# Attention phase of a fused two-layer block: norms moved to ScalarE, loads of x pinned, weight stores set apart

## The chip, the cores and the metric

The program runs on one core of a Trainium2 chip. A core has TensorE (PE in the profile; its weight loads are listed as PEld), VectorE (DVE), ScalarE (ACT), GpSimd (POOL) and SyncE (SP), each with its own instruction queue that is worked off in order, and 16 DMA engines that all queues share. The metric is the time on the device in microseconds (us); lower is better. All data is float32.

## The reference, cut to what matters

Eight batches of 512 tokens with 512 features go through four residual blocks. This case touches the first two.

```python
# B=8 batches, S=512 tokens, D=512; 16 heads of 32; context of 64 tokens per batch
x = x + tanh(g_xattn[0]) * L0_xattn(layernorm(x), ctx, Wq, Wg, bg, Wkv, Wo)
x = x + tanh(g_ffn[0])   * L0_ffn(layernorm(x), proj1, b1, proj2, b2)
x = x + tanh(g_xattn[1]) * L1_xattn(layernorm(x), ctx, mask)
x = x + tanh(g_ffn[1])   * L1_ffn(layernorm(x), gate_weight, gate_up, down, ...)

def layernorm(x): return (x - mean(x)) / sqrt(var(x) + 1e-5)

def L0_xattn(query, kv, ...):          # linear attention
    q = features(query @ Wq.T); gate = sigmoid(query @ Wg.T + bg)
    k, v = split(kv @ Wkv.T);   k = features(k)   # x+1 where x>0, else exp(x)
    summary = einsum('bhsd,bhse->bhde', k, v); k_sum = k.sum(tokens)
    attn = (q @ summary) / (q @ k_sum + 1e-6)
    return attn * gate @ Wo.T
def L0_ffn(x, ...): return gelu(x @ proj1.T + b1) @ proj2.T + b2   # 512 -> 2048 -> 512
```

## The kernel before

The program is one long, fully unrolled list of instructions. A scheduler of the framework orders each engine's instructions by a simulation, unless the kernel pins them: the set `in_order` names the engines whose instructions, as long as they are in it, are kept behind the one traced last on the same engine (class `Ordered`, line 47 on). After the set-up (line 1321) TensorE, VectorE and ScalarE leave the set; GpSimd and SyncE stay in program order all through the attention phase.

**Matrix products** are done by a scheme with seven block products in place of eight (numbered 1 to 7). A product with a weight needs the four blocks of the weight and three differences of them, and likewise of the activations: `combining` (line 243) makes the weight's differences in place on VectorE or GpSimd, `token_combinations` (line 614) those of the normed tokens. `Unit.step(m)` issues one product of 8 matmuls (1.73 us) into an accumulator bank of PSUM and then the work that takes it out (`after`).

**Attention phase** (loop over b from line 1331). Per batch it traces seven products of `QUp` (query), seven of `GUp` (gate), and seven of `ODown` (output projection) of the batch before, since the two last products of a unit are issued late, after the first of the next unit (`steps`). Between them stand `denominators` (the products `pd`, a reciprocal in two halves, a store of `z` to DRAM as `over`, and its spreading load `spread` back over partitions), `numerators` (the 32 small matmuls `pn`, which fill four banks), `gated` (the tile `th`) and `attended` (the tile `a`, then its three combinations).

**Normed tokens.** While batch b is worked on, the generator `prep` of batch b+1 is pulled step by step by `some(prep)`. It is `normed` (line 463): bn_stats and bn_aggr for four tiles of 128 tokens, `var`, then `rstd` by a power on GpSimd (line 480), a yield; then for each tile the norm (`xn`, line 491, VectorE), its turning by four transposes on TensorE (`pt`, line 500), the copy to `xnT` by ScalarE (line 503), a yield. In the attention phase the first pull is at the fourth step of the gate's products, the others at steps 0, 1, 3 and 5 of ODown's.

**x's loads.** `load_x` (line 153) loads 1 MB of x for a batch. For batches 2 to 7 the queue is ScalarE's (line 164). They are traced at step 1 of the gate's products of the batch two before. `store_x` (line 173) writes the result of the attention back.

**Weights of the feed-forward blocks** are made during earlier phases by builders, generators that are pulled beside the products. `build_first` runs on GpSimd in the attention phase, one pull in two of five steps (`tick`); `build_second` runs on VectorE in the first feed-forward phase, one pull per up product, from line 440. Per tile: load raw weights, wait `LAND` pulls, combine in place, store, wait `GAP` pulls. For the down weights `combining_again` (line 370) takes a second level of differences in place: it stores three quarters at once (`keep`), then changes the tile step by step, and stores each changed quarter after its step. All these tiles share one buffer (`build_tile`). SyncE issues their loads and stores in program order with all other loads.

**Last batch.** At b = 7 the steps of `ODown(6)` also carry `gated` (steps 1 and 2) and `attended` (step 4) of batch 7, whose output projection follows at once, and the norms and turnings of the first feed-forward batch, pulled at steps 4, 5 and 6.

The order around the change at the end of a batch:

```python
for n, (u, m) in enumerate(steps([ODown(done[0])] if done else [])):
    u.step(m)
    in_order.discard("tensor")
    if b < B - 1:
        next(den, None)
        if n == 6:
            spread(b)
    elif n in (1, 2):
        gated(b, g.th, n - 1)
    elif n == 4:
        attended(b, g.th, pn)
    if n in ((0, 1, 3, 5) if b < B - 1 else (4, 5, 6)):
        some(prep)
    tick()
```

Of the kernel before, what the change touches and what calls it, by code (L numbers as in the profile page):

```python
# [68 lines left out]
def flamingo_kernel(  # L69
# [24 lines left out]
    nc = SimpleNamespace(**{e: Ordered(tc, e, in_order) for e in in_order})  # L94
    stack = ctx.enter_context
# [57 lines left out]
    def load_x(ph, b):  # L153
        if ph == "xa0" and b % 4 == 3:
            t = awork.tile([P, NT, D], F32, tag="x4", name=f"x_{ph}{b}")
        else:
            t = work.tile([P, NT, D], F32, tag="x", name=f"x_{ph}{b}", bufs=3)
        if ph == "xa0":
            src = x[ts(b, S), :].rearrange("(t p) d -> p t d", p=P)
        else:  # L160
            src = between[ph, b]

        queue = nc.scalar if ph == "xa0" and b > 1 else nc.sync
        queue.dma_start(out=t, in_=src)
        xs[ph, b] = t
# [204 lines left out]
    def combining_again(ph, i, t, eng):  # L370


        b = t.rearrange("p k n (h q) -> p k n h q", q=P)
        b11, b12, b21, b22 = (b[:, :, n, h] for n in range(2) for h in range(2))

        def keep(m, w):
            nc.sync.dma_start(out=stream[ph][:, :, SPLIT_INNER.index(m), i, :], in_=w)

        sub = ALU.subtract
        for m, w in ((1, b11), (2, b21), (3, b22)):  # L380
            keep(m, w)
        eng.tensor_tensor(b12, b12, b11, sub)
        yield
        keep(5, b12)
        eng.tensor_tensor(b22, b22, b12, sub)
        yield
        keep(6, b22)
        eng.tensor_tensor(b21, b21, b22, sub)
        yield
        keep(4, b21)  # L390
        eng.tensor_tensor(b11, b22, b11, sub)
        yield
        keep(7, b11)
# [5 lines left out]
    def build_first():  # L399
# [10 lines left out]
        for i in range(4):  # L410
# [13 lines left out]
            yield from combining_again("ff0", i, t, nc.gpsimd)  # L424
# [13 lines left out]
    LAND, GAP = 11, 6  # L438

    def build_second():  # L440
# [10 lines left out]
        for i in range(SPLIT_CHUNKS["ff1"]):  # L451
# [5 lines left out]
            yield from in_place(combining_again("ff1", i, t, nc.vector))  # L457
# [5 lines left out]
    def normed(ph, b, tag, normed_part=lambda t: None):  # L463
# [4 lines left out]
        ordered = ph == "ff0" and b > 1  # L468
        if ph == "xa0" or ordered:
            in_order.add("vector")  # L470
        for t in range(NT):
            st = small.tile([P, 6], F32, tag="st", name=f"st_{tag}_{t}")
            nc.vector.bn_stats(st, xb[:, t, :])
            nc.vector.bn_aggr(mv[:, t, :], st)
        if b:
            in_order.discard("vector")
        var = small.tile([P, NT], F32, tag="var", name=f"var_{tag}")
        nc.vector.tensor_scalar(var, mv[:, :, 1], LN_EPS, None, ALU.add)  # L478
        rstd = small.tile([P, NT], F32, tag="rstd", name=f"rstd_{tag}")
        nc.gpsimd.tensor_tensor(rstd, var, neg_half, ALU.pow)  # L480
        if ph in ("xa0", "ff0") or tag.startswith("ff1"):
            yield
# [4 lines left out]
        def norm(t):  # L487
            xn[t] = work.tile([P, D], F32, tag="xn", name=f"xn_{tag}_{t}")
            if ordered:
                in_order.add("vector")  # L490
            nc.vector.tensor_scalar(
                xn[t], xb[:, t, :], mv[:, t, 0:1], rstd[:, t : t + 1], ALU.subtract, ALU.mult
            )
            if ordered:
                in_order.discard("vector")
# [19 lines left out]
        if ordered:  # L515
            norm(0)
            yield
        for t in range(NT):
            if not ordered:
# [811 lines left out]
    for b in range(B):  # L1331
# [4 lines left out]
        for n, (u, m) in enumerate(steps([q])):  # L1336
# [5 lines left out]
            if n == 4:  # L1342
                flush()
            tick()
# [26 lines left out]
        for n, (u, m) in enumerate(steps([ODown(done[0])] if done else [])):  # L1371
            u.step(m)
# [5 lines left out]
            elif n in (1, 2):  # L1378
                gated(b, g.th, n - 1)
            elif n == 4:  # L1380
                attended(b, g.th, pn)
            if n in ((0, 1, 3, 5) if b < B - 1 else (4, 5, 6)):
                some(prep)
            tick()
        for _ in prep:
# [188 lines left out]
```

## Time and profile before

| What | Value |
|---|---|
| Median of three runs (lowest, highest) | 2095.27 us (2091.73, 2095.57) |
| The profiled execution, its time on the device | 2096.49 us |
| The same execution, span from first to last instruction | 2094.7 us |
| Busy: PE, PEld, DVE, ACT, POOL | 2053.7, 1821.1, 1511.3, 610.8, 171.1 us |
| Mean granted PE clock | 0.992 |
| Attention phase, from PE's first projection of x to the first product of the feed-forward block | 54.27 to 409.16 us |
| DVE `xn_xa` (line 491), 28 times between 54.27 and 353.58 | 33.9 us, mean 1232 ns |
| DVE bn_stats, bn_aggr there, 28 each | mean 667 and 181 ns |
| POOL `rstd_xa` there, 7 times | mean 1009 ns |
| POOL waits for stores of `build_ff_down` | 46.1 us, 3 times |

The busy times add up over engines that work side by side; only what PE waits for, or what runs while its granted clock is below 1, sets the end here. A line of the timeline gives the start in us, the duration, the engine, the line in the kernel, the operation, what it writes and reads, its shape and count, and in brackets how long the engine had been idle before it and what ended that. Where a helper records the instruction, its line is 60. "q" after an engine's name marks its instruction queue, for issues of DMA.

### The profile page before, as it was taken

What the parts mean: (1) busy time and instruction counts of PE and PEld (TensorE: products, weight loads), DVE (VectorE), ACT (ScalarE), POOL (GpSimd) and SP (SyncE); (2) the same over time, 40 slices, a digit from 0 to 9 for tenths busy, and PEclk for the clock granted to TensorE, in tenths of its full rate; (3) what the DMA queues carried; (4) which work ended last, traced back from release to release, by engine and by line L of the source; (5) the groups of instructions that cost most, each with busy time, mean ns of one, the idle gap of its engine ahead of it and who ended that gap; (6) DMA issues with size and microseconds to landing.
All of it is one profiled execution on the core that took longest, in us unless ns stands there. A gap on an engine that the chain in (4) does not pass through costs nothing.

```text
span 2094.7 us, 35097 instructions
## 1 busy us (share of the span) xinstructions
PE 2053.7 (98%) x12796; PEld 1821.1 (87%) x12796; DVE 1511.3 (72%) x2965; ACT 610.8 (29%) x1264; POOL 171.1 (8%) x164
## 2 busy tenths in 40 slices
PE   8999999999999999999999999999999999999998
PEld 4777887799999898989988989898989889898988
DVE  3688888657768576768767687777777676876758
ACT  3433333232332324232334222312222222223121
POOL 3233320100000000000001010000000010100000
PEclk9999999999999999999999999999999999999999
DMA  7354763598888887879786858586766858585865
GB/s 227 127 177 147 208 210 98 159 302 283 261 285 296 271 288 262 283 240 310 249 305 214 286 162 284 190 269 211 238 224 208 270 174 291 159 283 163 269 203 170
DMA packets 304170, 484.66 MB, mean 231 GB/s; under 512 B 36992, under 2 KB 103712, under 8 KB 299904
## 3 DMA queue, kind: packets, MB, share of 16 engines
q1 hardware_dynamic: 296560, 455.65, 68.2%
q10 hardware_dynamic: 5856, 23.20, 2.9%
q0 software_dynamic: 1584, 3.57, 0.7%
q8 instruction: 103, 1.69, 0.3%
q14 instruction: 67, 0.55, 0.1%
HBM read 413.04 MB, written 69.27 MB: 230 GB/s over the span
## 4 chain that ended last, share of the span: by engine, by line
PE 90%; DVE 4%; DMA 3%; issue 1%; POOL 1%; ACT 0%; SPq 0%; ACTq 0%; DVEq 0%; POOLq 0%
PE x_ff L840 26%; PE w_ff L840 13%; PE x_ff_down L1035 13%; PE w_ff_down L1035 8%; PE z_ff L840 6%; PE z_ff_down L1035 4%; PE v_ff_down L1035 4%; PE x_xa_down L956 2%; PE x_q L840 2%; PE pt_ff L500 1%; PE x_g L840 1%; PE pt_xa L500 1%; PE w_xa_down L956 1%; PE w_g L840 1%; DMA stream_ff<-build_ff_down 1%
## 5 line engine op out<-in xcount | busy, mean ns | idle before, releaser
L840 PE MATMUL w_ff<-S_ff,w_ff 128*128 128x256 f32 x1280 | 305.4, 381 | 4.2 <-DVE a_ff L895 4.2
L840 PE MATMUL x_ff<-S_ff,w_ff 128*128 128x256 f32 x1280 | 304.3, 380 | 0.0
L840 PE MATMUL x_ff<-xnT_ff,w_ff 128*128 128x256 f32 x1280 | 294.6, 379 | 0.0
L852 ACT COPY u_ff<-x_ff 128x512 f32<-128x512 f32 x240 | 140.0, 584 | 477.7 <-PE x_ff L840 453.1
L840 PEld LDWEIGHTS x_ff<-S_ff,w_ff 128*128 128x128 f32 x1280 | 240.5, 190 | 40.1 <-issue 5.0
L840 PEld LDWEIGHTS w_ff<-S_ff,w_ff 128*128 128x128 f32 x1280 | 240.0, 191 | 37.4 <-DVE a_ff L895 5.0
L840 PEld LDWEIGHTS x_ff<-xnT_ff,w_ff 128*128 128x128 f32 x1280 | 237.7, 190 | 31.1 <-ACT u_ff L852 0.5
L1035 PE MATMUL x_ff_down<-w_ff_down,split_ff_down 128*128 128x128 f32 x1344 | 157.9, 275 | 0.0
L1035 PEld LDWEIGHTS x_ff_down<-w_ff_down,split_ff_down 128*128 128x128 f32 x1344 | 153.9, 192 | 0.0
L840 PE MATMUL z_ff<-xnT_ff,w_ff 128*128 128x256 f32 x640 | 152.6, 381 | 0.0
L840 PEld LDWEIGHTS z_ff<-xnT_ff,w_ff 128*128 128x128 f32 x640 | 120.7, 192 | 15.8
L1049 DVE TENSOR_TENSOR part_ff_down<-part_ff_down 128x128 f32<-128x128 f32 x315 | 84.7, 288 | 64.5 <-ACT part_ff_down L1062 57.6
L1035 PE MATMUL w_ff_down<-w_ff_down,split_ff_down 128*128 128x128 f32 x896 | 105.3, 275 | 0.0
L1035 PEld LDWEIGHTS w_ff_down<-w_ff_down,split_ff_down 128*128 128x128 f32 x896 | 102.6, 192 | 0.0
L895 DVE TENSOR_TENSOR a_ff<-w_ff,u_ff 128x512 f32<-128x512 f32 x64 | 43.9, 687 | 69.6 <-ACT u_ff L852 69.5
L900 ACT ACTIVATE a_ff<-a_ff,b_sb 128x256 f32<-128x256 f32 x128 | 58.1, 501 | 97.6 <-DVE a_ff L895 97.6
L923 DVE SCALAR_TENSOR_TENSOR g_ff<-th_ff,x_ff 128x512 f32<-128x512 f32 x48 | 32.9, 685 | 70.3 <-ACT th_ff L922 70.3
L480 POOL TENSOR_TENSOR rstd_ff<-var_ff,neg_half 128x4 f32<-128x4 f32 x15 | 15.3, 1020 | 826.5 <-DVE var_ff L478 826.5
L1035 PE MATMUL w_ff_down<-w_ff_down,s_ff 128*128 128x128 f32 x672 | 81.5, 275 | 0.0
L1035 PE MATMUL x_ff_down<-w_ff_down,a_ff 128*128 128x128 f32 x672 | 80.4, 275 | 0.0
L1035 PEld LDWEIGHTS w_ff_down<-w_ff_down,s_ff 128*128 128x128 f32 x672 | 79.4, 192 | 0.8
L1035 PEld LDWEIGHTS x_ff_down<-w_ff_down,a_ff 128*128 128x128 f32 x672 | 78.4, 192 | 0.5
(254 smaller groups left out, 3450.4 us busy)
## 6 DMA issues: line engine op xcount, KB each, us to landing
w_ff_down<-stream_ff SPq DMA_DIRECT2D x680, 256.0 KB
w_ff<-ff_up SPq DMA_DIRECT2D x560, 256.0 KB
stream_ff<-build_ff_down SPq DMA_DIRECT2D x49, 448.0 KB
x_ff<-x_ff SPq DMA_DIRECT2D x16, 1024.0 KB
share<-shares SPq DMA_DIRECT2D x64, 256.0 KB
ff_up<-build_ff_up SPq DMA_DIRECT2D x42, 256.0 KB
spread<-over SPq DMA_DIRECT2D x32, 256.0 KB
x_ff<-x_xa ACTq DMA_DIRECT2D x8, 1024.0 KB
```

The costliest lines, as they stand in the source:

```text
L480: nc.gpsimd.tensor_tensor(rstd, var, neg_half, ALU.pow)
L500: nc.tensor.transpose(pt[:, c, :], xn[t][:, ts(c, P)], ident)
L840: nc.tensor.matmul(p[:, n, :], lhsT=w[:, c, ts(n, P)], rhs=moving, **self.mark(m, 2 * n + c),)
L852: nc.scalar.copy(self.s[m], p)
L895: nc.vector.tensor_tensor(h, p, s, ALU.add)
L900: nc.scalar.activation(h[:, n, :], p[:, n, :], AF.Gelu, bias=b1_sb[:, f : f + 1])
L923: nc.vector.scalar_tensor_tensor(g, th, 1.0, p, ALU.add, ALU.mult)
L956: nc.tensor.matmul(p[:, t, :], lhsT=a[:, k, ts(t, P)], rhs=w[k // 2][:, k % 2, :], **self.mark(m, 2 * k + t),)
L1035: nc.tensor.matmul(p[bank][:, place, :], lhsT=operand[k][:, c, :], rhs=w[at // 4][:, ts(at % 4, P)], start=bank not in opened, stop=True, ...
L1049: return lambda: nc.vector.tensor_tensor(m(k), m(k), m(by), ALU.add)
```

## The change

- `here(*engines)` pins instructions of these engines in program order for as long as its block lasts.
- `load_x` issues under `here("scalar")`.
- `combining_again` takes a number `apart`: after the first three stores so many pulls pass before the first change in place (2 in `build_first`, 8 in `build_second`), and the four stores of the changed quarters come together at the end. `LAND` and `GAP` go from 11 and 6 to 10 and 5.
- `normed`: for batches 1 to 7 of the attention phase and the first feed-forward batch the norm is an Identity activation on ScalarE with `rstd` as scale and a new `shift` (minus the mean times `rstd`, a multiply on VectorE and one on GpSimd) as bias. For the former the norm of tile t+1 is traced before the turning of tile t and pinned, which takes one more pull; statistics are pinned on VectorE only in batch 0 (and in feed-forward batches from 2 on, as before).
- The main loop pulls `prep` once more, at step 4 of the query's products. At the last batch `gated` moves to steps 4 and 5 and `attended` to step 6 of ODown's products, VectorE is pinned from step 4 to the end of them, and `prep` is pulled at step 6 alone.

```diff
@@ -92,6 +92,15 @@
 ):
     in_order = {"tensor", "vector", "scalar", "gpsimd", "sync"}
     nc = SimpleNamespace(**{e: Ordered(tc, e, in_order) for e in in_order})
+
+    @contextmanager
+    def here(*engines):
+
+        new = {*engines} - in_order
+        in_order.update(new)
+        yield
+        in_order.difference_update(new)
+
     stack = ctx.enter_context
 
     const = stack(tc.tile_pool(name="const", bufs=1))
@@ -161,7 +170,8 @@
             src = between[ph, b]
 
         queue = nc.scalar if ph == "xa0" and b > 1 else nc.sync
-        queue.dma_start(out=t, in_=src)
+        with here("scalar"):
+            queue.dma_start(out=t, in_=src)
         xs[ph, b] = t
 
     stores = []
@@ -367,30 +377,29 @@
         for q in range(7):
             nc.sync.dma_start(out=store[ph, i, q], in_=t[q])
 
-    def combining_again(ph, i, t, eng):
+    def combining_again(ph, i, t, eng, apart):
 
 
         b = t.rearrange("p k n (h q) -> p k n h q", q=P)
         b11, b12, b21, b22 = (b[:, :, n, h] for n in range(2) for h in range(2))
 
-        def keep(m, w):
-            nc.sync.dma_start(out=stream[ph][:, :, SPLIT_INNER.index(m), i, :], in_=w)
+        def keep(*of):
+            for m, w in of:
+                nc.sync.dma_start(out=stream[ph][:, :, SPLIT_INNER.index(m), i, :], in_=w)
 
         sub = ALU.subtract
-        for m, w in ((1, b11), (2, b21), (3, b22)):
-            keep(m, w)
+        keep((1, b11), (2, b21), (3, b22))
+        for _ in range(apart):
+            yield
         eng.tensor_tensor(b12, b12, b11, sub)
         yield
-        keep(5, b12)
         eng.tensor_tensor(b22, b22, b12, sub)
         yield
-        keep(6, b22)
         eng.tensor_tensor(b21, b21, b22, sub)
         yield
-        keep(4, b21)
         eng.tensor_tensor(b11, b22, b11, sub)
         yield
-        keep(7, b11)
+        keep((5, b12), (6, b22), (4, b21), (7, b11))
 
     def placed(ph, t):
 
@@ -421,7 +430,7 @@
                     yield
             if i < 3:
                 up = load_up(i + 1)
-            yield from combining_again("ff0", i, t, nc.gpsimd)
+            yield from combining_again("ff0", i, t, nc.gpsimd, 2)
             yield
         streamed.add("ff0")
 
@@ -435,7 +444,7 @@
                 return
             yield
 
-    LAND, GAP = 11, 6
+    LAND, GAP = 10, 5
 
     def build_second():
         for i in range(6):
@@ -454,7 +463,7 @@
             for _ in range(LAND):
                 yield
             yield from in_place(combining(nc.vector, placed("ff1", t)))
-            yield from in_place(combining_again("ff1", i, t, nc.vector))
+            yield from in_place(combining_again("ff1", i, t, nc.vector, 8))
             for _ in range(GAP + 2):
                 yield
         streamed.add("ff1")
@@ -465,19 +474,23 @@
         xb = xs[ph, b]
         xnT = work.tile([P, NC, S], F32, tag="xnT", name=f"xnT_{tag}")
         mv = small.tile([P, NT, 2], F32, tag="mv", name=f"mv_{tag}")
-        ordered = ph == "ff0" and b > 1
-        if ph == "xa0" or ordered:
-            in_order.add("vector")
-        for t in range(NT):
-            st = small.tile([P, 6], F32, tag="st", name=f"st_{tag}_{t}")
-            nc.vector.bn_stats(st, xb[:, t, :])
-            nc.vector.bn_aggr(mv[:, t, :], st)
-        if b:
-            in_order.discard("vector")
+        held = ph == "ff0" and b > 1
+        by_scalar = ph == "xa0" and b > 0 or tag == "ff0_0"
+        ahead = held or ph == "xa0" and b > 0
+        with here(*(["vector"] if held or ph == "xa0" and b == 0 else [])):
+            for t in range(NT):
+                st = small.tile([P, 6], F32, tag="st", name=f"st_{tag}_{t}")
+                nc.vector.bn_stats(st, xb[:, t, :])
+                nc.vector.bn_aggr(mv[:, t, :], st)
         var = small.tile([P, NT], F32, tag="var", name=f"var_{tag}")
         nc.vector.tensor_scalar(var, mv[:, :, 1], LN_EPS, None, ALU.add)
         rstd = small.tile([P, NT], F32, tag="rstd", name=f"rstd_{tag}")
+        if by_scalar:
+            shift = small.tile([P, NT], F32, tag="nshift", name=f"nshift_{tag}")
+            nc.vector.tensor_scalar(shift, mv[:, :, 0], -1.0, None, ALU.mult)
         nc.gpsimd.tensor_tensor(rstd, var, neg_half, ALU.pow)
+        if by_scalar:
+            nc.gpsimd.tensor_tensor(shift, shift, rstd, ALU.mult)
         if ph in ("xa0", "ff0") or tag.startswith("ff1"):
             yield
         if tag.startswith("ff1"):
@@ -486,13 +499,15 @@
 
         def norm(t):
             xn[t] = work.tile([P, D], F32, tag="xn", name=f"xn_{tag}_{t}")
-            if ordered:
-                in_order.add("vector")
-            nc.vector.tensor_scalar(
-                xn[t], xb[:, t, :], mv[:, t, 0:1], rstd[:, t : t + 1], ALU.subtract, ALU.mult
-            )
-            if ordered:
-                in_order.discard("vector")
+            with here(*(["vector", "scalar"] if ahead else [])):
+                if by_scalar:
+                    nc.scalar.activation(
+                        xn[t], xb[:, t, :], AF.Identity, bias=shift[:, t : t + 1], scale=rstd[:, t : t + 1]
+                    )
+                else:
+                    nc.vector.tensor_scalar(
+                        xn[t], xb[:, t, :], mv[:, t, 0:1], rstd[:, t : t + 1], ALU.subtract, ALU.mult
+                    )
 
         def turn(t):
             pt = psum(f"pt_{tag}_{t}").rearrange("p (c q) -> p c q", q=P)
@@ -512,11 +527,11 @@
                     norm(t + 2)
                 yield
             return xnT
-        if ordered:
+        if ahead:
             norm(0)
             yield
         for t in range(NT):
-            if not ordered:
+            if not ahead:
                 norm(t)
             elif t + 1 < NT:
                 norm(t + 1)
@@ -1341,6 +1356,8 @@
                 load_x("ff0", 0)
             if n == 4:
                 flush()
+                if b < B - 1:
+                    some(prep)
             tick()
         if done:
             attended(done[0], done[2], numerators(*done[0:2]))
@@ -1369,19 +1386,22 @@
             spread(b)
             pn = numerators(b, q.q)
         for n, (u, m) in enumerate(steps([ODown(done[0])] if done else [])):
+            if b == B - 1 and n == 4:
+                in_order.add("vector")
             u.step(m)
             in_order.discard("tensor")
             if b < B - 1:
                 next(den, None)
                 if n == 6:
                     spread(b)
-            elif n in (1, 2):
-                gated(b, g.th, n - 1)
-            elif n == 4:
+            elif n in (4, 5):
+                gated(b, g.th, n - 4)
+            elif n == 6:
                 attended(b, g.th, pn)
-            if n in ((0, 1, 3, 5) if b < B - 1 else (4, 5, 6)):
+            if n in ((0, 1, 3, 5) if b < B - 1 else (6,)):
                 some(prep)
             tick()
+        in_order.discard("vector")
         for _ in prep:
             pass
         done = b, q.q, g.th
```

More of the change, by code (lines that the diff above doesn't have):

```diff
@@ L11 @@
 import math
-from contextlib import ExitStack
+from contextlib import ExitStack, contextmanager
 from types import SimpleNamespace
```

## The prediction

> **What bounds the kernel now.** I read the page first: PE is busy 2053.7 of 2094.7 us and 90% of the chain of waits is PE. So an edit can win only what PE stands idle or runs at a lower granted clock. Next I cut the span into stretches: the start up to PE's first projection of x (54.27), then one stretch for each batch of the attention phase, from one `pn` product (numerators) to the next, and the rest.
>
> ```profile
> 0.00:54.27 54.27, 44.23 (x172) 24.46 (x172) 17.87 (x51) 18.92 (x46) 18.22 (x27) 0.91 0.74 229
> 54.27:95.48 41.21, 38.24 (x176) 30.73 (x176) 26.74 (x41) 17.08 (x32) 11.60 (x9) 0.96 0.21 67
> 95.48:142.64 47.16, 42.79 (x226) 33.57 (x225) 37.23 (x51) 14.74 (x27) 14.98 (x9) 1.00 0.65 196
> 142.64:183.07 40.43, 40.43 (x225) 33.71 (x225) 33.70 (x52) 14.29 (x27) 8.35 (x6) 1.00 0.57 183
> 183.07:227.32 44.25, 42.18 (x225) 34.95 (x225) 34.72 (x49) 14.51 (x27) 16.12 (x10) 0.96 0.64 196
> 310.12:353.58 43.46, 40.76 (x226) 33.62 (x225) 35.13 (x52) 14.22 (x27) 4.99 (x3) 1.00 0.39 116
> 353.58:409.16 55.58, 50.82 (x290) 40.09 (x290) 46.24 (x82) 13.72 (x26) 7.04 (x10) 0.97 0.37 116
> ```
>
> The columns are stretch, length, busy us (count) of PE, PE's weight loads, DVE, ACT, POOL, then granted clock, DMA share, GB/s. The batch of 142.64 to 183.07 has no PE gap: 40.43 us is what PE needs. The others hold the same 225 or 226 products and take 47.16, 44.25, 42.36, 40.44 and 43.46: 6.7, 3.8, 1.9, 0.0 and 3.0 us more, 15.5 in all. DVE is busy some 34 of 40 us, ACT 14.
>
> What PE waits for in these stretches (waits of PE, 54.27 to 409: total, times, longest) and how one looks in the timeline (start, duration, engine, operation, then the idle time before it and what ended it):
>
> ```profile
> PE pt_xa L500 <- DVE xn_xa L491: 11.8, 8, 2.4
> PE x_xa_down L956 <- DVE x_xa L972: 4.0, 3, 1.7
> PE pt_ff L500 <- DVE a L1224: 2.2, 1, 2.2
> ```
> ```profile
> 325.84 1.01 POOL L60 TENSOR_TENSOR rstd_xa<-var_xa,neg_half 128x4 f32<-128x4 f32 x1 [13.78 <-DVE var_xa L478]
> 326.82 2.07 POOL L60 TENSOR_TENSOR build_ff_down<-build_ff_down 128x896 f32<-128x896 f32 x1
> 326.88 2.75 DVE L491 TENSOR_SCALAR xn_xa<-x_xa,mv_xa,rstd_xa 128x512 f32<-128x512 f32 x2 [1.12 <-POOL rstd_xa L60]
> 329.23 0.66 PE L500 MATMUL pt_xa<-ident,xn_xa 128*128 128x128 f32 x4 [2.35 <-DVE xn_xa L491]
> ```
>
> The statistics end at 325.4, rstd at 326.85, the first norm 2 us later because POOL combines weights at the same time, and PE has run out of other work. Two more places cost time.
>
> ```profile
> 29.26 0.39 ACTq L164 DMA_DIRECT2D x_xa<-in_x  x1
> 29.70 0.59 ACT L60 COPY v<-pv 128x512 f32<-128x512 f32 x1 [8.36 <-DMA w_o<-in_wo]
> 30.82 5.81 PE L60 MATMUL pk<-w_k,ctxT 128*128 128x512 f32 x8 [4.52 <-ACT ctxT L60]
> ```
> ```profile
> 880.85 2.63 SPq L60 DMA_DIRECT2D stream_ff<-build_ff_down  x3
> 891.18 1.09 DVE L60 TENSOR_TENSOR build_ff_down<-build_ff_down 128x896 f32<-128x896 f32 x1 [7.66 <-DMA stream_ff<-build_ff_down]
> 892.93 3.78 PE L840 MATMUL w_ff<-S_ff,w_ff 128*128 128x256 f32 x8 [3.89 <-DVE a_ff L895]
> ```
>
> First: a load of x for a batch that is needed some 100 us later was scheduled into ACT's queue in the start, held ACT for 8.36 us until a weight transfer had landed, and so PE for 4.52. Another such load stands at 0.75. Second: DVE combines a tile in place, must wait until the store that reads it has landed, and everything behind it on DVE, PE's `w` bank included, waits too.
>
> **What the skill says.** The Trainium skill, "TensorE: Matmul & The Clock Gate", What's actually happening: a gate halves PE's clock after an idle window of about 3.4 us. The trace agrees: the granted clock is 0.50 in 28.26:35.09, 79.46:82.87, 202.34:205.75, 390.08:393.49 and 891.84:898.67, each after one of these gaps, and half of PE's busy time there (4.27, 3.41, 3.41, 3.41, 5.74) is lost. "SBUF — State Buffer", Who interferes with whom: a DVE tensor_scalar in a two-port mode and a GpSimd operation block each other for a whole instruction, and "PE and ACT never wait on anyone". The trace agrees: `xn_xa` on DVE takes 442 ns at least, 1479 in the median, 2296 at most. "ScalarE: Activation LUTs", Table sets: identity is in every table set; the trace shows table loads at 1.25 and 415.57 and none between, so the new activation should add none. "DMA: Bandwidth & Descriptors", Issuing engines are not separate DMA queues: loads issued by ACT and SP share the 16 DMA engines; the trace has them 93% busy in the first 25 us.
>
> **The change, part by part.**
>
> *x's loads pinned.* Six issues of 0.41 us (L164) stay on ACT's queue. The two early ones move behind ACT's work for the late q product, near 66 and 105 us, where DMA share is 0.21 and 0.65. In the start PE's gap of 4.52 goes, and the half clock after it (4.27/2 = 2.13): 6.65. Late next is PE itself, since w_q and w_g are in place long before use (DVE reads w_q at 39.98). Besides, 1 MB less competes with the first context and w_k: PE waits 3.41 at 8.09 for `ctx`. The gain lies between 0 (w_k bounds anyway) and 3.4; I take 1.5. Sum 8.1. The four later loads now issue some 6 us later than at 183.70, when x's store (177.05, 6.57 us) has landed; the 2.6 us that ACT waited there goes. They pass the copies and activations of one product, and are read some 28 us later.
>
> *Statistics sooner.* Per batch 4 x (667 + 181) ns of bn_stats and bn_aggr, var (248) and one new small multiply (like var) on DVE, the pow (1.01) and a new multiply on POOL (1.0 by the same row). They move from the fourth step of g to the fifth of q: six products of 1.73 and the 1.07 of `pn` earlier, 11.4 us. They pass DVE's four `a` (0.68 each) and three combinations (0.69), which become 3.7 us later; these end at 319.70 and PE reads them at 323.99, 4.3 us later, so that is covered, barely. On POOL the pow passes one or two builder steps; I traced the builder's ticks, and it falls behind a combining whose store or load was issued 10 us or more earlier, in every batch.
>
> *Norms on ACT.* DVE loses 28 operations, 33.9 us busy over seven batches. ACT gains 28: the price of the page on ScalarE (What ACT_TABLE_LOAD costs) is an estimate of 186 + 2 x 93 + 0.833 x 512 = 798 ns, about 0.7 back to back; the nearest row, an activation of 128x512, took 631. ACT goes from 14.4 to some 17.4 of 40.4 us. With the first norm a step ahead of its turning, `pt_xa` has nothing to wait for: 20 us at most over the rows (15.5, and in 54.27:95.48 gaps of 2.22 and 0.75 with 1.7 of half clock, 4.7). What is late next is DVE's x_xa read (1.66 at 259.13), where DVE now has 5 us more room. I take 13 and 4 of them, the rest for new collisions.
>
> *POOL's stores apart.* Two builder steps more per tile and the four late stores at the end: 61 of 64 ticks instead of 53. POOL's waits for stores (46.1 us, 3 times) shrink, and SP no longer stands between combinations with the store of `z` behind it. But the last four combinations (2.1 us each) move from 307-329 to about 345-355, beside the last batch on DVE: cost 0 to 3.
>
> *Last row.* ff0's first norms move to ACT (0.55 each off DVE), turnings later, gating in DVE's order ahead of the reads of the last products. The gating waits for `spread`, which lands at 386.4 (issued 377.0); DVE then holds the read of bank x behind it, which PE needs at 383.08. Against that the 2.2 and 0.84 us gaps and 1.7 of half clock at 390 may go. Between -3 and +5; I take 0.
>
> *ff1's builder.* The eight steps apart (13.8 us of products) exceed the 10.3 us from issue at 880.85 to 891.18: 3.89 + 5.74/2 = 6.8 goes. LAND and GAP shorter: combining starts one product, 1.73, sooner after its load; the shortest room where the order stays within a row was 420.63 to 431.36, 10.7 us, and DVE waited for no load. I deduct 0.5. The steps add up to 213 of 224 (207 before).
>
> Sum: 8.1 + 4 + 13 + 0 + 6.3 = 31.4. The profiled execution took 2096.5 for a span of 2094.7; 2065.1 after it. The median of the runs is 1.2 lower: 2064.
>
> **Rivals.** *A wait replaced:* the start and half of the ff1 stall win (6.65 + 3.4), but in the rows the four `a` come late, or the scheduler puts turnings elsewhere, and only 5 of 20 us is won: 15 in all, 2080. For it: DVE's 34 of 40 us and the slack of 4.3; against: 142.64:183.07 and 269.68:310.12 show that this DVE load already fits behind PE.
> *ACT held (slower):* the pinned norm stands in ACT's queue ahead of the copies of u that free PE's banks. If rstd and its product come later than ACT by more than two products (3.5 us), PE stops: 4 us and 1.7 of half clock in seven batches, 40 us, against 20 of old waits gone and 14.4 won elsewhere: +5, 2101. For it: POOL waited 27.5 us once for a store, with rstd behind it; against: the 11.4 us of lead.
> *It does nothing:* the scheduler finds the same waits elsewhere, 2095.
>
> **How the numbers follow.** Chances: forecast 0.66 (2053 to 2074), wait replaced 0.22 (2074 to 2088), nothing 0.03, slower 0.09. Best end: 6.65 + 3.4 + 20.2 + 6.8 + 3 = 40 off, 2055, less 2 for the spread of the runs: 2053. The upper end takes in most of the second case: 2083. About 0.2% (4.2 us) is what a measurement can tell from no change. Faster 0.88, same 0.03, slower 0.09.
>
> **What would show it.** No L164 issue before 60 us, `pk` without its 4.5 us wait; batch stretches near 40.4; `xn_xa` on ACT near 0.7 us with no PE wait on it; no DVE wait on `stream_ff`; clock 0.50 gone after 28, 79, 202 and 891. I would be wrong if ACT's waits for POOL's `nshift` exceed 3 us, if PE waits for `a` or `s_xa`, if DVE waits for `in_gu` loads, or if the last stretch grows past 60 us.

## The result, and the profile after

The changed kernel takes 2091.89 us (median of 22 runs, 2087.42 to 2097.62), the kernel before 2096.38 (22 runs): ratio 0.9982, interval 0.9974 to 0.9990. It is faster by 4.5 us where 31 were forecast, and lies outside the forecast range of 2053 to 2083. The span of the profiled execution went from 2094.7 to 2090.0.

The windows of the trace after, cut at the same marks as before (stretch, length, busy us of PE, weight loads, DVE, ACT, POOL, granted clock, DMA share, GB/s):

```profile
0.00:61.22 61.22, 45.74 (x173) 25.79 (x173) 19.70 (x61) 19.15 (x46) 22.55 (x32) 0.86 0.65 195
61.22:99.19 37.97, 36.83 (x176) 30.16 (x176) 22.76 (x38) 19.48 (x36) 9.66 (x9) 1.00 0.22 73
99.19:142.45 43.26, 41.84 (x226) 33.68 (x225) 32.82 (x50) 17.06 (x31) 13.35 (x9) 1.00 0.72 227
309.36:354.19 44.83, 42.63 (x226) 34.68 (x225) 31.12 (x37) 17.21 (x31) 15.06 (x8) 0.96 0.51 153
354.19:412.70 58.51, 51.38 (x289) 40.88 (x289) 46.93 (x83) 16.69 (x30) 7.21 (x11) 0.91 0.52 146
```

Read the lengths and the clock: the start has become 7 us longer at a mean clock of 0.86 (0.91 before), the last stretch 2.9 longer at 0.91 (0.97 before). Set side by side, in us, with the best version found below (batch 1's statistics pinned, GpSimd held behind `a`):

| stretch | before | after | forecast gain | gain | best version |
|---|---|---|---|---|---|
| start, to the first product with w_q | 54.27 | 61.22 | 8.1 | -6.95 | 44.04 |
| first, to the first `pn` | 41.21 | 37.98 | 4 | 3.23 | 36.86 |
| six rows, `pn` to `pn` | 258.09 | 254.99 | 13 | 3.10 | 244.32 |
| last row | 55.58 | 58.52 | 0 | -2.94 | 58.96 |
| first feed-forward phase | 674.94 | 667.59 | 6.3 | 7.35 | 667.59 |
| the rest | 1010.6 | 1009.7 | 0 | 0.9 | 1009.7 |
| sum | 2094.7 | 2090.0 | 31.4 | 4.7 | 2061.5 |

Three places show why. **The start**, from the timeline after (start, duration, engine, operation, idle time before it and what ended it):

```profile
27.92 1.35 SPq L60 DMA_DIRECT2D x_xa<-in_x  x1
38.83 0.69 DVE L483 BATCH_NORM_STATS2 st_xa<-x_xa 128x6 f32<-128x512 f32 x1 [15.72 <-DMA x_xa<-in_x]
39.44 0.28 DVE L60 TENSOR_TENSOR ksum<-pkv,heads 128x128 f32<-128x128 f32 x1
39.87 0.87 PE L60 MATMUL pkv<-v,k 64*128 64x160 f32 x2 [12.18 <-DVE ksum L60]
```

These are the statistics of batch 1. The change took them out of VectorE's hand-kept order, and the scheduler put them into the set-up, ahead of `ksum`. There they wait for batch 1's x, VectorE stands 15.72 us, and PE, whose bank `ksum` reads, 12.18. The granted clock is 0.50 for 17.07 us from 30.65 on.

**A row**, the one that begins at 266.45; first the same three combinations in the kernel before (its row begins at 269.68):

```profile
274.74 0.69 DVE L879 TENSOR_TENSOR s_xa<-a 128x512 f32<-128x512 f32 x1
275.46 0.69 DVE L880 TENSOR_TENSOR s_xa<-s_xa,a 128x512 f32<-128x512 f32 x1
276.07 0.69 DVE L881 TENSOR_TENSOR a<-a 128x512 f32<-128x512 f32 x1
```
```profile
268.04 6.63 POOL L60 TENSOR_TENSOR build_ff_down<-build_ff_down 128x896 f32<-128x896 f32 x3 [22.29 <-DMA stream_ff<-build_ff_down]
...
273.10 2.12 DVE L894 TENSOR_TENSOR s_xa<-a 128x512 f32<-128x512 f32 x1
...
274.64 3.38 POOL L60 TENSOR_TENSOR raw_up<-raw_up,raw_up 128x512 f32<-128x512 f32 x2
275.26 1.64 DVE L895 TENSOR_TENSOR s_xa<-s_xa,a 128x512 f32<-128x512 f32 x1
...
276.82 1.75 DVE L896 TENSOR_TENSOR a<-a 128x512 f32<-128x512 f32 x1
278.49 0.68 DVE L1156 TENSOR_TENSOR qs_q<-w_q,u_q 128x512 f32<-128x512 f32 x1
...
279.20 0.63 ACT L620 ACTIVATE fe_q<-qs_q 128x512 f32<-128x512 f32 x1 [6.01 <-DVE qs_q L1156]
...
279.74 0.57 ACT L867 COPY u_g<-x_g 128x512 f32<-128x512 f32 x1
...
280.36 1.99 PE L855 MATMUL x_g<-S_xa,w_g 128*128 128x256 f32 x8 [2.21 <-ACT u_g L867]
```

Read the second view from the bottom. PE waits for the copy of `u_g`, which frees its bank. ScalarE made that copy late because `fe_q` stands ahead of it and waits for `qs_q`. On VectorE `qs_q` stands behind three combinations that take 5.5 us in place of 2.1, and GpSimd combines weights at the same time. No wait for a turning (`pt_xa`) is left over 0.3 us: the old wait went, and this one took its place.

**The last row**:

```profile
387.03 2.50 DVE L60 SCALAR_TENSOR_TENSOR th<-th,spread 128x512 f32<-128x512 f32 x4 [5.60 <-DMA spread<-over]
389.44 0.75 DVE L60 SCALAR_TENSOR_TENSOR x_xa<-x_xa_down,gates_half,x_xa 128x512 f32<-128x512 f32 x1
...
390.24 2.08 PE L971 MATMUL x_xa_down<-w_o,a 128*128 128x256 f32 x4 [6.75 <-DVE x_xa L60]
```

The read of PE's bank stands behind the gating, and the gating waits for `spread`.

### The profile page after: what moved, and what is told of

Its sections match the earlier page's. It is cut to its first block, busy times and chain, and to the rows that moved or that the text cites. A ratio compares the mean times of both kernels' runs of the same rounds, so it can differ in the third digit from the quotient of the medians.

```text
span 2090.0 us, 35123 instructions
## 1 busy us (share of the span) xinstructions
PE 2050.6 (98%) x12796; PEld 1820.7 (87%) x12796; DVE 1488.7 (71%) x2941; ACT 629.4 (30%) x1294; POOL 172.0 (8%) x172
## 4 chain that ended last, share of the span: by engine, by line
PE 90%; DVE 5%; DMA 2%; ACT 1%; SPq 1%; issue 1%; POOL 0%; ACTq 0%; DVEq 0%; POOLq 0%
PE x_ff L855 26%; PE w_ff L855 13%; PE x_ff_down L1050 13%; PE w_ff_down L1050 8%; PE z_ff L855 7%; PE z_ff_down L1050 4%; PE v_ff_down L1050 4%; PE x_xa_down L971 2%; PE x_q L855 2%; PE pt_ff L515 1%; PE pt_xa L515 1%; PE x_g L855 1%; PE w_xa_down L971 1%; SPq L60 1%; PE pst L675 1%; PE pr L720 1%
```

## The experiments

Stretches come from one profiled execution each. "The seven stretches" are the first and the six rows of the table (299.3 us before, 293.0 after). "Pinned" means kept in the order of the program text, "free" means placed by the scheduler. Ratios are to the kernel before. Kernels with the same order in the rows differ there by 3 to 4 us (the kernel before with only the second builder changed took 303.1 for the seven), so less than that in a single stretch sum says little.

### Undoing or doing one part

*Statistics kept in VectorE's order for all batches:*

```diff
-        with here(*(["vector"] if held or ph == "xa0" and b == 0 else [])):
+        with here(*(["vector"] if held or ph == "xa0" else [])):
```

> The kernel after, with the statistics of batches 1 to 7 kept in VectorE's order again where they are traced; nothing else. Theory (in the set-up the statistics of batch 1 stand in VectorE's queue before their x has come, and ksum and PE's pkv behind them): PE's gap of 12.18 us at 27.69 and the half clock behind it are gone, the start goes from 61.22 to 46 to 49 us, the total from about 2092 to 2077 to 2081. Rival (the pinned loads make x come late and the start waits for DMA anyway): the start stays above 57 us, the total above 2087.

Measured: start 43.86, total only 2089.37 (ratio 0.9964, 0.9950 to 0.9978). The start is 17.4 us shorter, more than the theory asked; the rival, which wanted it above 57, falls. But the total misses the theory's range by 8 us, since the seven stretches sum to 307.4 in place of 293.0, with waits for `u_g` of up to 6.00 us. So statistics that are pinned 11.4 us sooner have a price in the rows, which the forecast had called covered.

*The last row as before* (gating at steps 1 and 2, `attended` at 4, pulls at 4, 5, 6, no pinning):

> The kernel after, with the last row (gating, attended, pulls of the norms) placed as in the kernel before. Theory (VectorE holds the read of PE's bank behind a gating that waits for the spread): the gap of 6.75 us at 383.49 and half of the 10.24 us at half clock go, against 2 to 3 us of waits that the row had before; the last stretch goes from 58.52 to 53 to 56 us, the total by 3 to 6 us down. Rival (the spread lands late for other reasons and sets the row in either order): the stretch stays within 1 us of 58.5.

Measured: 2089.97 (0.9966, 0.9957 to 0.9976), last stretch 56.27, just outside what was expected; the total is 1.9 us less than that of the kernel after, or 3.3 by the ratios. The gap of 6.75 is gone, but one of 3.94 stands in its place, for a turning that waits for `a`.

*The first builder's stores as before:*

```diff
-            yield from combining_again("ff0", i, t, nc.gpsimd, 2)
+            yield from combining_was("ff0", i, t, nc.gpsimd)
```

> The kernel after, with the first builder's second level of combining and its stores as in the kernel before (no steps apart, each store right after its step). Theory (its later combinations on GpSimd fall beside VectorE's a and their combinations in the rows of batches 5 and 6 and slow them, so ScalarE's copies of u come late): PE's two gaps of 2.2 us at 278 and 321 go, these rows come back to 40.4 to 41.5 us (from 42.91 and 44.83), the total by 3 to 5 us down. Rival (the norms pinned on ScalarE hold its queue, whatever GpSimd does): both rows stay above 42.5 us.

Measured: 2089.55 (0.9963, 0.9952 to 0.9975). The two rows are 41.67 and 42.73, between theory and rival, and waits for `u_g` of 2.0 us stand at 195 and 323. Inconclusive: a third row has become longer (44.40, from 42.35), and the seven stretches sum to 291.9 in place of 293.0. The stores move GpSimd's bursts from row to row; by this run they are neither the cause nor cleared. The last stretch is 56.17, 2.35 shorter, though its order is that of the kernel after.

*The kernel before with only the second builder changed:*

> The kernel before, with only the second builder as in the kernel after (eight steps apart, its late stores at the end, LAND 10, GAP 5). Theory (VectorE's wait for the store that reads the tile is what cost PE 3.89 us and the half clock in the first feed-forward phase): 674.94 us of that phase become 667 to 669, the total goes down 6 to 8 us. Rival (the gain of that phase in the kernel after came from its changed start, not from the builder): less than 2 us.

```profile
413.82:1081.41 667.59, 667.59 (x4474) 624.26 (x4473) 464.93 (x980) 209.84 (x442) 7.69 (x7) 1.00 0.87 283
```

Measured: the phase takes 667.59, to the hundredth what the kernel after takes, and PE is busy in all of it; total 2089.44 (0.9964, 0.9952 to 0.9977). The theory holds. Eight steps apart and the shorter LAND and GAP weren't tried one by one.

*The kernel before with only x's loads pinned:*

> The kernel before, with only the loads of x kept in ScalarE's order where they are traced. Theory (the early load in ScalarE's queue held v's copy and PE): the start goes from 54.27 to 44 to 47 us, the rest of the program stays, the total goes down 7 to 11 us. Rival (the start's gain needs the norms or statistics of the change as well): the start stays above 50 us.

```profile
0.00:44.04 44.04, 40.62 (x173) 22.85 (x173) 17.87 (x51) 18.94 (x46) 18.19 (x27) 1.00 0.75 223
```

Windows of that run, the start: 10.23 us shorter than before, clock 1.00 all through. In the start the loads gain what was forecast and 2 us more. The total, 2090.13 (0.9970, 0.9958 to 0.9981), is only 6.9 us below the kernel before, a little under the theory's 7 to 11, since the seven stretches take 302.5 (299.3 before), a difference that lies within their noise.

### Where the rows' gain went

*Only batch 1's statistics pinned* (`ph == "xa0" and b <= 1`):

> The kernel after, with the statistics of batch 1 alone kept in VectorE's order; those of batches 2 to 7 stay free. Theory (two faults of different signs: batch 1's statistics too early cost the start 17 us, and the pinned statistics of later batches cost the rows 13 us in the run where all were pinned): the start is 43.5 to 45 us, the seven stretches between numerators sum to 290 to 295 us as in the kernel after (293.0) and not 307 as with all pinned, the total is 2072 to 2078. Rival (a start that is 17 us sooner itself shifts the stores and GpSimd's work into the rows, so the rows grow whatever the statistics do): the rows sum to 301 us or more, the total is above 2083.

Measured: 2075.73 (0.9897, 0.9881 to 0.9914), start 43.59, stretches 296.1: as the theory has it, 1 us over its range. This one condition is worth 16 us.

*All statistics pinned, but pulled at the fourth step of g as before, the first norm at the sixth* (besides the pinning of all statistics, as above):

```diff
-                if b < B - 1:
-                    some(prep)
...
-            if n == 3 or n > 3 and not done:
+            if n == 3 or n == 5 and b < B - 1 or n > 3 and not done:
```

> The kernel after, with all statistics kept in VectorE's order and pulled at the fourth step of g again as in the kernel before (behind a and its combinations), and the first norm on ScalarE pulled at the sixth step of g. Theory (statistics ahead of a delay qs_q, ScalarE's fe_q and, behind it, the copy of u_g that PE waits for): the start is 43.5 to 45 us, the seven stretches sum to 285 to 293 us, PE's waits for u_g stay under 4 us in sum, the total is 2066 to 2076. Rival (a and its combinations are late because GpSimd combines beside them, wherever the statistics stand): u_g waits of 2 us remain in at least three rows and the sum is 295 us or more.

Measured: 2069.78 (0.9870, 0.9854 to 0.9887), stretches 288.0, no wait for `u_g`. The theory's numbers, but not yet its reason, for GpSimd has moved too. Its timeline in this run:

```profile
305.19 1.01 POOL L60 TENSOR_TENSOR rstd_xa<-var_xa,neg_half 128x4 f32<-128x4 f32 x1 [30.32 <-DVE nshift_xa L490]
306.28 0.20 POOL L60 TENSOR_TENSOR nshift_xa<-nshift_xa,rstd_xa 128x4 f32<-128x4 f32 x1
306.46 2.63 POOL L60 TENSOR_TENSOR build_ff_down<-build_ff_down 128x512 f32<-128x512 f32 x2
```

GpSimd stands 30 us at the power, until the statistics are done, 14 us after `pn` (291.4) and behind VectorE's combinations (the last from 298.2 to 298.9). Only then does it go on with the weights. In the kernel before it does the same (20.01 us ahead of the power at 282.91). In the kernel after the free statistics run about a row early: the last of the seven powers is at 285.33, against 325.84 before. The power no longer stands between `pn` and the combinations, and GpSimd starts when a store has landed (22.29 us ahead of 268.04), 1.6 us after `pn`. The waits of GpSimd in the seven stretches (total, times, longest), before and after, show the same change:

```profile
POOL rstd_xa L60 <- DVE var_xa L478: 125.2, 6, 34.2
POOL build_ff_down L60 <- DMA stream_ff<-build_ff_down: 46.1, 3, 27.5
```
```profile
POOL build_ff_down L60 <- DMA stream_ff<-build_ff_down: 95.3, 4, 25.4
POOL rstd_xa L60 <- DVE var_xa L486: 28.6, 4, 9.6
POOL rstd_xa L60 <- DVE nshift_xa L490: 21.7, 2, 21.1
```

*That kernel with the last row and the first builder's stores as before:*

> As the run with the statistics later and pinned, and besides the last row and the first builder's stores as in the kernel before. If the causes add up: 3 to 6 us less than that run, 2062 to 2071, with the last stretch at 54 to 56 us and no PE wait for the spread. If the last row and GpSimd's stores are two names for one loss: within 2 us of that run.

Measured: 2073.42 (0.9887, 0.9870 to 0.9903), neither case: 3.6 us more. The last stretch is 55.50, but the six rows went from 249.7 to 257.2. With two pulls less per tile other steps stand ahead of the power, and a burst falls beside `a` again (170.72 to 177.35, from 1.4 us after `pn` on, ahead of the power at 185.12).

*The same with GpSimd's stores left apart, and then with one pull in the last row:*

> As the run with the statistics later and pinned, with the last row (gating, attended, pulls of the norms) as in the kernel before, and GpSimd's stores apart as in the kernel after. Theory (the last row and the stores are separate causes, of opposite sign: the stores apart gain in the rows once the power stands late in GpSimd's queue, 249.8 us against 257.2 in six rows): 2 to 4 us less than the run with the statistics later, 2065 to 2068, the last stretch 54.5 to 56.5 us. Rival (the stores apart and the old last row collide at the end): within 1 us of it or above.

> As the run before it, but of the norms of the first feed-forward batch only one is pulled in the last row (at step 6, as in the kernel after). If the early turnings are what makes PE wait 2.2 us for a: 2 to 3 us less than that run. If PE has to wait for a at the next product anyway: within 1 us.

Measured: 2068.91 (0.9870, 0.9853 to 0.9886) and 2069.58 (0.9869, 0.9852 to 0.9885). The rows are back at 249.7 and 250.6: the stores apart are worth 4.5 us here. The old last row gives 0.9 us, under its forecast and not clear of noise (the ratio is 0.9870 with either order); the pulls give nothing.

*The power traced one pull later*, first with only batch 1's statistics pinned, then with all pinned early:

```diff
+        if ph == "xa0" and b:
+            yield
         nc.gpsimd.tensor_tensor(rstd, var, neg_half, ALU.pow)
...
-        if ph in ("xa0", "ff0") or tag.startswith("ff1"):
-            yield
...
+        if (ph == "xa0" and not b) or ph == "ff0" or tag.startswith("ff1"): yield
```

> As the run with batch 1's statistics alone pinned, but the power and the shift's multiply on GpSimd are traced one pull later (at the fourth step of g, with the first norm), the statistics on VectorE as there. Theory (the power is a gate in GpSimd's queue: the weights' combinations behind it can't start before the statistics are done; traced sooner, it lets them fall beside VectorE's a and s_xa, which makes ScalarE's copy of u late): the overlap of GpSimd with s_xa falls from 5.0, 2.2, 3.7 us in the worst rows to under 1.5, the seven stretches sum to 286 to 291 us and not 296.1, total 2067 to 2072. Rival (the place of the statistics on VectorE is what counts): sum 294 or more, total 2074 or more.

> As the run with all statistics pinned at the fifth step of q, but the power and the shift's multiply traced one pull later, as in the run beside this one. Theory (pinned statistics ahead of a cost too: a comes 3.7 us later and the power, though traced later, finds its input ready and holds nothing back): the seven stretches sum to 296 to 306 us (307.4 there), PE still waits for u_g 2 us or more in three rows, total 2077 to 2088. Rival (only the place of the power in GpSimd's queue counts): sum 286 to 291 us, total 2067 to 2072.

Measured: 2078.53 (0.9912, 0.9895 to 0.9929), stretches 298.6: a miss. The numbers are those of the rival, for which the place of the statistics counts; but the test did not do what it was meant to do. The power's place in the queue alone doesn't hold GpSimd back, as its timeline shows:

```profile
252.67 2.07 POOL L60 TENSOR_TENSOR build_ff_down<-build_ff_down 128x896 f32<-128x896 f32 x1 [31.48 <-DMA stream_ff<-build_ff_down]
254.70 1.45 POOL L60 TENSOR_TENSOR rstd_xa<-var_xa,neg_half 128x4 f32<-128x4 f32 x1
```

The free statistics were ready long before, so the power went through at once. The second run took 2092.86 (0.9976, 0.9967 to 0.9986), stretches 310.3: worse than both cases, on the theory's side.

So the test had to hold GpSimd by something that comes at the right time in any case. *One multiply of 128x4 on GpSimd, which reads the last combination of `a`, on the version with only batch 1's statistics pinned:*

```diff
         combine_inner(slice(0, 2), "x")
+        gate = small.tile([P, NT], F32, tag="gate", name=f"gate_{b}")
+        nc.gpsimd.tensor_tensor(gate, a[:, 1, 0, 0, 0:4], neg_half, ALU.mult)
```

> As the run with batch 1's statistics alone pinned, with one small multiply (128x4) on GpSimd after each a and its combinations, which reads the last combination: GpSimd's later work can't start before them. Statistics, power and norms as there. Theory (what the rows lost is GpSimd's combinations beside VectorE's a and s_xa; in the kernel before, and in the run with the statistics later, the power's wait for late statistics held them back by chance): GpSimd beside s_xa falls to under 1.5 us in every row, waits for u_g are gone, the seven stretches sum to 286 to 292 us (296.1 there), total 2066 to 2073. Rival (the statistics' place on VectorE or the norms on ScalarE make the rows long): sum 294 or more.

Measured: 2062.88 us (0.9833, 0.9817 to 0.9850), stretches 281.2, below the theory's own range. Windows, timeline and GpSimd's longest wait of this run:

```profile
122.79:163.22 40.43, 40.43 (x226) 33.71 (x225) 28.33 (x44) 17.32 (x31) 12.28 (x11) 1.00 0.51 159
163.22:203.65 40.43, 40.43 (x226) 33.71 (x225) 33.19 (x49) 17.09 (x31) 12.74 (x9) 1.00 0.59 180
203.65:244.08 40.43, 40.43 (x226) 33.71 (x225) 30.40 (x46) 17.20 (x31) 9.62 (x9) 1.00 0.65 204
244.08:284.51 40.43, 40.43 (x226) 33.70 (x225) 30.11 (x43) 17.11 (x31) 15.30 (x11) 1.00 0.53 131
```
```profile
249.97 0.69 DVE L894 TENSOR_TENSOR s_xa<-a 128x512 f32<-128x512 f32 x1
...
250.69 0.69 DVE L895 TENSOR_TENSOR s_xa<-s_xa,a 128x512 f32<-128x512 f32 x1
251.31 0.68 DVE L896 TENSOR_TENSOR a<-a 128x512 f32<-128x512 f32 x1
...
252.07 0.20 POOL L60 TENSOR_TENSOR gate<-a,neg_half 128x4 f32<-128x4 f32 x1 [30.25 <-DVE a L896]
...
252.22 9.14 POOL L60 TENSOR_TENSOR build_ff_down<-build_ff_down 128x896 f32<-128x896 f32 x4
...
254.09 0.59 ACT L867 COPY u_g<-x_g 128x512 f32<-128x512 f32 x1 [0.83 <-PE x_g L855]
...
257.28 1.28 DVE L483 BATCH_NORM_STATS2 st_xa<-x_xa 128x6 f32<-128x512 f32 x2
```
```profile
POOL gate L60 <- DVE a L896: 150.3, 6, 30.3
```

Four rows stand at 40.43 with PE busy in all of it. The combinations take 0.69 each again, `u_g` waits for nothing but PE, and GpSimd's 9 us of weights come right behind. The six rows gain 13.8 us against the kernel before, where 13 were forecast. Added up from the timelines, GpSimd works beside the three combinations for 5.2, 3.9, 4.9 and 3.6 us in the last four of the six rows of the kernel after, and for none in any of the six rows of the kernel before, of the run with the statistics later, and of this run. (In the run that this one is built on, the burst of the last of the six falls beside `th` instead: 6.78 us for its four parts in place of 2.50.) So the theory is shown: the rows lost their gain to GpSimd's work beside `a`'s combinations, in one row beside `th`, and without it they gain what was forecast. Two things are not shown. The norms' move was never tried without the other parts in the rows (the stores apart alone were worth 4.5 us above), and the multiply was not tried on the kernel before, where the power already held GpSimd.

*The same multiply with all statistics pinned early:*

> As the run with all statistics pinned at the fifth step of q, with the same small multiply on GpSimd behind a. If the statistics ahead of a cost by themselves (a 3.7 us later, qs_q and u_g behind it): the seven stretches sum to 295 to 303 us (307.4 there), PE waits for u_g in three rows. If GpSimd alone was the cause: 286 to 292 us, no wait for u_g over 1 us.

Measured: 2073.41 (0.9881, 0.9864 to 0.9897), stretches 293.8, 1.2 us below the first case. Four of the six rows are at 40.43 to 42.52, within 0.7 us of the run before, though the statistics stand ahead of `a` in them too. Two are 44.90 and 47.36. The timeline of the longer one:

```profile
296.75 1.01 POOL L60 TENSOR_TENSOR rstd_xa<-var_xa,neg_half 128x4 f32<-128x4 f32 x1 [26.70 <-ACT qs_q L1158]
...
297.99 2.94 POOL L60 TENSOR_TENSOR raw_up<-raw_up,raw_up 128x512 f32<-128x512 f32 x2
```
```profile
298.49 1.31 DVE L894 TENSOR_TENSOR s_xa<-a 128x512 f32<-128x512 f32 x1
299.73 1.75 DVE L622 SCALAR_TENSOR_TENSOR q<-qs_q,fe_q 128x512 f32<-128x512 f32 x1
...
303.32 0.63 ACT L620 ACTIVATE fe_q<-qs_q 128x512 f32<-128x512 f32 x1 [5.23 <-DVE qs_q L1156]
...
305.84 1.65 PE L855 MATMUL x_g<-S_xa,w_g 128*128 128x256 f32 x3 [3.88 <-ACT u_g L867]
```

The small multiply holds only what stands behind it. With statistics done early the power goes through 6.5 us after `pn` (290.26), and two combinations between it and the multiply slip in beside `s_xa` and `q`: 1.31 + 1.75 in place of 2 x 0.69, 1.68 us of delay. PE's waits of 2.51 and 3.88 less this leave 0.8 and 2.2 for the statistics. That is worked out and not shown by a run of its own; the run lies between its two cases, nearer to "GpSimd alone" in four rows of six.

### The last row once more

On the version with batch 1's statistics pinned and GpSimd held, first the whole last row as before, then only the pinning left out:

> As the run with batch 1's statistics pinned and GpSimd held behind a, with the last row (gating, attended, pulls of the norms) as in the kernel before. Theory (VectorE's pinned gating in front of the read of PE's bank costs the last row 2 to 3 us): the last stretch goes from 58.96 to 55.5 to 57 us, the gap of 5.92 us for x_xa is gone, total 2058 to 2061. Rival (the last row waits for the spread in either order): stretch within 1 us, total 2062 or more.

> As that base run, but only VectorE's pinning in the last row is left out; gating and attended stay at steps 4, 5 and 6. If the pinning makes the gap: it goes as with the whole last row undone (stretch 55.5 to 57 us). If the later place of the gating makes it: stretch within 1 us of 58.96.

Measured: 2065.66 (0.9847, 0.9833 to 0.9860) with a last stretch of 58.74, and 2062.85 (0.9835, 0.9820 to 0.9850) with 58.71; the base had 58.96. The theory of the first run falls and its rival holds; in the second the pinning falls as the cause, and the later place of the gating, its other case, has fallen with the first run. Without the pinning another wait stands in the row:

```profile
362.53 2.49 DVE L1213 SCALAR_TENSOR_TENSOR th<-th,spread 128x512 f32<-128x512 f32 x4
364.93 2.47 DVE L1239 TENSOR_TENSOR a<-th,pn 128x512 f32<-128x512 f32 x4
365.76 1.23 PE L515 MATMUL pt_ff<-ident,xn_ff 128*128 128x128 f32 x8 [3.94 <-DVE a L1239]
```

PE waits for the read of its bank behind the gating, or for `a`, which also stands behind the gating. The old order made this stretch 1.9 to 2.8 us shorter in three other pairings and not here. The order isn't all of it in any case: with the order of the kernel after, the stretch lies between 56.17 (the first builder's stores as before) and 59.45 (all statistics pinned, GpSimd held).

The traces show one thing that all four runs with the small multiply share and no other has. From the base run:

```profile
335.49 4.66 POOL L60 TENSOR_TENSOR build_ff_down<-build_ff_down 128x896 f32<-128x896 f32 x2
```
```profile
338.13 2.04 DVE L490 TENSOR_SCALAR nshift_ff<-mv_ff 128x4 f32<-128x4 f32 x1
```

GpSimd's held burst now falls beside VectorE's small multiply `nshift_ff`, which takes 2.04 us, up to the end of the burst, in place of 0.16 in the kernel after. The `z` behind it comes 2 us later, and so does the last load of `spread` (25.71 us after `pn`, against 23.61 in the kernel after). How much of the old order's gain this takes was not tried in a run of its own.

## Why the prediction was wrong

- *x's loads pinned, 8.1:* right, 10.23 on the kernel before. Beside the 6.65 of the sum, PE's wait of 3.41 for `ctx` went and 1.30 of smaller waits came (0.68 for `ctxT`, 0.62 for w_k), and a second stretch at half clock, 7.78 to 11.19, went too. The prediction had put 1.5 for the first and nothing for the second.
- *ff1's builder, 6.3:* right, 7.35; the deduction of 0.5 for LAND and GAP wasn't needed.
- *Norms on ACT, 4 and 13:* the mechanism was right. The norm takes 0.80 us on ScalarE (estimate 0.798), the waits for turnings are gone, and with GpSimd held these stretches gain 4.35 and 13.8, the other parts included. In the changed kernel it was 3.23 and 3.10.
- *Statistics sooner* is the step that failed. It read how far they move, 11.4 us, and not that the diff takes the pinning from them for every batch but the first. Free, batch 1's went into the set-up and cost 17 us there (61.22 against 43.86 and 43.59 with them pinned), and the others' ran about a row early. So what it said of the four `a` ("covered, barely") was not put to the test in the changed kernel. Where all statistics are pinned early and GpSimd is held, it holds in four rows of six; in the other two PE waits for ScalarE's copy of `u_g`, whose slack is used up sooner than the 4.3 us of PE that the step used.
- *On POOL the pow passes one or two builder steps:* this part of the same step looked at when the power gets done, not at what its wait had held back. That wait kept the weights off VectorE's two-input combinations; holding GpSimd by other means is worth 12.9 us (2075.73 to 2062.88). The Trainium skill, "SBUF — State Buffer", Who interferes with whom, says that a VectorE instruction with two SBUF inputs contends with a GpSimd instruction that reads SBUF, and one with a single SBUF input, outside the two-port modes, doesn't. The prediction used that page for the norms alone. The traces agree on both halves: `s_xa` goes from 0.69 to 1.64 and 2.12 beside GpSimd, while bn_stats takes 0.64 each beside it (1.28 for two at 257.28), as without it (1.28 at 281.48 after).
- *POOL's stores apart, 0:* GpSimd's waits for stores were to shrink from 46.1 us. They grew to 95.3 in the seven stretches: where the power no longer held GpSimd, the stores did.
- *Last row, 0 (-3 to +5):* the loss of 2.94 is just inside the range, and the wait is the one named there.
- *The clock:* half clock as such is as the prediction has it, but the length of a gap doesn't tell when it comes. In the kernel before 3.41 us at 0.50 follow the gaps of 2.22 (ended at 77.48) and 2.07 (201.29), shorter than the idle window that it cites, and none follows the gap of 2.35 (329.23).
- Of the rivals, "a wait replaced" was right that a new wait takes the old one's place, but not on what: in the row shown the combinations are late, and the four `a` take 2.47 us as elsewhere. "ACT held" named the copies of u as what PE would wait for, but with the pinned norm ahead of them; there it is `fe_q`, and no norm of the rows waited for `nshift`. No rival had the start on the other side of zero.

The version with batch 1's statistics pinned and GpSimd held behind `a` takes 2062.88 us, 1.7% less than the kernel before. That it lies where the forecast of 2064 lay is partly luck: the start, ff1 and the rows gave 2.1, 1.1 and 1.1 us more than their terms, the last row 3.4 less.

## What to carry to other kernels

When an edit drops a pin, ask where the scheduler may now put the instruction, and what stands behind it in its queue while its input isn't there. Before moving an instruction that waits, ask what its wait was holding back; if that is useful, make it a dependence of its own, as one small operation did here, and see what the held work falls beside then. Price a delay on one engine by the first queue that feels it, not by the read of the bound engine alone.

## What the runs showed of the hardware

GpSimd's multiply of 128x4 takes 0.20 us, the power of the same size 1.01; the forecast had taken 1.0 for both. VectorE's `a` (one input from PSUM, one from SBUF) takes its usual 0.62 each beside GpSimd (2.47 for four at 270.60), so in that row the cost falls on the combinations that follow it. Other VectorE operations pay as well: `q` 1.75 in place of 0.69, `th` 6.78 for four in place of 2.50, and the small multiply `nshift_ff`, which reads a single tile, 2.04 in place of 0.16. Why that one pays and bn_stats doesn't is not shown.
